# The place of each row's greatest entry, found through 22 segment maxima and one gathered segment

## The chip, the cores and the metric

One core of one Trainium2 chip runs the whole program in one launch. The metric is the device time of a run in microseconds (us), the median over repeated runs. Engines are written as in the profile: PE multiplies matrices (PEld loads its weights), DVE, ACT and POOL work on vectors, SP issues transfers, and POOL also issues the indirect transfers (gathers by a list of rows).

## The reference

The input is a table `x` of 2708 rows by 512 and a matrix `adj` of 2708 by 2708, all float32. Four layers follow one another, each with a layer norm and relu before it and `x` added after it. Only layers 0 and 1 matter for this change:

```python
h = jnp.maximum(_layernorm(x, axis=-1), 0.0)
# layer 0
mask = adj > 0
head = mask / jnp.maximum(jnp.sqrt(jnp.sum(mask * mask, -1, keepdims=True)), 1e-12)
inc = adj + head
x = x + (inc @ h) / jnp.sum(inc, -1, keepdims=True)
# layer 1, with h computed anew from x
a = jnp.maximum(adj, jnp.eye(n))
atts = queries @ keys.T / key_dim ** 0.5        # for each of 8 heads
atts = softmax(atts - 1e16 * (1.0 - a))
x = x + sum_over_heads(atts @ values @ Wo)
# layer 2: two graph convolutions with adj, relu, relu, then tanh of a product
# layer 3: the mask adj != 0 times a projection, over the column sums of the mask
```

Most entries of `adj` are zero, the others lie between 0.05 and 5.42, and the first rows and columns hold most of them. Layer 1's mask is multiplied by 1e16, so that in a row whose greatest and second greatest entries of `max(adj, I)` differ enough, the softmax is 1 at the place of the greatest entry and 0 elsewhere. The layer is then a lookup: each row takes the projected row that its greatest entry points to.

## The kernel before, in words

The rows are worked in 22 row tiles, 21 of 128 rows and a tail tile of 20. `tile_adj_preln_kernel` computes layer 0 in its first part, up to about 515 us; the layers after it have code of their own.

Layer 0 multiplies a dense first part of the adjacency by blocks, and gathers the rest. The rest of a row tile's columns is sparse, so the kernel finds which of them are non-zero at all (`count`, `rank_blocks`, `search`), fetches just these rows of the transposed adjacency by indirect transfers issued on POOL (`gather_adj`, L635, tiles `ac`), fetches the rows of the normalised table that belong to them (`gather_rows`, L654, tiles `h`), and lets PE add their products (L866, operands `inc` for dense blocks, `incl` for gathered ones). `incidence` makes these operands on DVE: L698 takes the mask part, L706 adds the entry.

`stats_to` runs ahead of PE. For each row tile it loads the tile's rows of `adj` whole (`load_slab`, a `slab` tile `ar` of 128 x 2708), forms the row's statistics with ACT (`row_norm`, `row_sum`: number of positive entries, sum, degree) and then calls `attended`, which finds the greatest and second greatest entry and the place of the greatest:

```python
nc.vector.tensor_max(ar[:n, cols], ar[:n, cols], ident[:n, :n])
nc.vector.max(tops[:n, m, :], ar[:n])
nc.vector.max_index(at_top[:n, m, :], tops[:n, m, :], ar[:n])
```

The first instruction puts the identity into the tile's diagonal block (L622), the second returns a row's eight greatest values (L623, MAX8), and the third the places of those eight (L624, which the profile shows as a load of the eight values, MATCH_VALUE_LOAD, and a search, FIND_INDEX8). Row tiles 0 to 5 (`LATE`) leave this out at first; their rows are loaded again in iterations 15 to 20 of the loop over row tiles, and `attended` is called one iteration after each load (L892-895).

`flags` (L278-288) later compares the two greatest values of each row and asks for a general attention path where they are too close; the rows of this input take the lookup. L914 copies the places into `idx`, by which layer 1's lookup gathers (L1172).

The main loop (L857-913) runs over the 22 row tiles: PE's sum, the scaling by the degree and the addition of `x` (L879), the layer norm of the result (`norm`, with the small operations L194 to L204), its transposition and projection one and two iterations later (`after`), then `stats_to` and `gathers_to` for tiles ahead. Each engine works its instructions in order, and POOL's gathers of all kinds share one queue. Tiles of the scratch pool have a set number of buffers; an instruction that writes one waits until the last reader of what was in it is done.

Of the kernel before, what the change touches and what calls it, by code (L numbers as in the profile page):

```python
# [9 lines left out]
FP = mybir.dt.float32  # L10
# [3 lines left out]
U32 = mybir.dt.uint32  # L14
U8 = mybir.dt.uint8
I32 = mybir.dt.int32
AF = mybir.ActivationFunctionType
ALU = mybir.AluOpType
AX = mybir.AxisListType
# [3 lines left out]
P = 128  # L23
LN_EPS = 1e-5
NORM_EPS = 1e-12
MASK_SCALE = 1e16
# [18 lines left out]
def kernel(  # L45
# [27 lines left out]
    nc = tc.nc  # L73

    N, D = x.shape
    H, _, DK = wk_d.shape
    NT = (N + P - 1) // P
    NFULL = N // P
# [4 lines left out]
    UNIT = 4  # L83
# [20 lines left out]
    ident = const.tile([P, P], FP, name="ident")  # L104
# [43 lines left out]
    idx = const.tile([P, NT], U32, name="idx")  # L148
# [16 lines left out]
    nc.gpsimd.memset(ones_b, 1.0)  # L165


    adj_units = bass.AP(adj_t.tensor, 0, [[UNIT, N * N // UNIT], [1, UNIT]])

    def span(t):  # L170
# [73 lines left out]
    with tc.tile_pool(name="l0_slab", bufs=2) as slabs, tc.tile_pool(  # L244
        name="l0_h", bufs=1
    ) as hp, tc.tile_pool(name="l0_w", bufs=2) as wp, tc.tile_pool(
        name="l0_acc", bufs=2, space=PSUM
    ) as ps_acc, tc.tile_pool(name="l0_small", bufs=1, space=PSUM) as ps_small, tc.tile_pool(
        name="l0_list", bufs=3, space=PSUM
    ) as ps_list, tc.tile_pool(name="l0_tr", bufs=1, space=PSUM) as ps_tr, tc.tile_pool(  # L250
        name="l0_y", bufs=1, space=PSUM
# [8 lines left out]

        idx_a = hp.tile([P, NT, NCH], U32, name="idx_a")

        tops = hp.tile([P, NT, 8], FP, name="tops")
        at_top = hp.tile([P, NT, 8], U32, name="at_top")
        cnts, sums_sgn, ends, caps = (
            hp.tile([P, NT], FP, name=name) for name in ("cnts", "sums_sgn", "ends", "caps")
        )
# [5 lines left out]
        if TAIL:  # L273
            nc.gpsimd.memset(tops[:, NFULL, :], 0.0)
            nc.gpsimd.memset(tops[:, NFULL, 0:1], 2.0)
            nc.gpsimd.memset(at_top[:, NFULL, :], 0)

        def flags():  # L278

            score = wp.tile([P, NT, 2], FP, name="score", bufs=1)  # L280
            nc.vector.tensor_scalar(
                score, tops[:, :, 0:2], 1.0, MASK_SCALE, op0=ALU.subtract, op1=ALU.mult
            )
            nc.vector.tensor_tensor(bad[:, :NT], score[:, :, 1], score[:, :, 0], ALU.is_ge)
            nc.vector.tensor_tensor(
                bad[:, BAD_NEG : BAD_NEG + NT], sums_sgn, cnts, ALU.not_equal
            )
            nc.vector.tensor_tensor(bad[:, BAD_MANY : BAD_MANY + NT], ends, caps, ALU.is_gt)
# [17 lines left out]
        nc.gpsimd.iota(place_i, pattern=[[P, NCH]], base=1, channel_multiplier=1)  # L306
        places = hp.tile([P, NCH], FP, name="places")
        nc.vector.tensor_copy(places, place_i)

        pending, pending_c = [], []  # L310

# [253 lines left out]
        def count_signs(m, last):  # L565

            sgn = slabs.tile([P, N], BF, name="sgn", bufs=GROUP)
            behind(sgn[:1, :1], last)
            nc.scalar.activation(sgn, slab[m], AF.Sign, accum_out=sums_sgn[:, m : m + 1])
            nc.scalar.activation(sgn, sgn, AF.Relu, accum_out=cnts[:, m : m + 1])  # L570
# [46 lines left out]
        def attended(m):  # L617

            n = rows(m)
            cols = slice(m * P, m * P + n)  # L620
            ar = slab.pop(m)
            nc.vector.tensor_max(ar[:n, cols], ar[:n, cols], ident[:n, :n])  # L622
            nc.vector.max(tops[:n, m, :], ar[:n])  # L623
            nc.vector.max_index(at_top[:n, m, :], tops[:n, m, :], ar[:n])  # L624

        gathers, gather_slot = {}, [0]

# [117 lines left out]
        normed, near, far = [0], [LEAD], [LEAD]  # L745
# [16 lines left out]
        def stats_to(m):  # L762


            while normed[0] <= order_n.index(m):
                t = order_n[normed[0]]
                do_next()
                load_slab(t)
                if normed[0] + 1 < NT:
                    load_slab(order_n[normed[0] + 1])  # L770
                row_norm(t)
                row_sum(t)
                if t == 0 or t % GROUP == GROUP - 1 or t >= NT - 2:
                    last_block = count(masks)
                    if t not in ZERO:
                        if dense_of(t):
                            rank_blocks(list(masks), last_block)
                        else:
                            flush_counts()
                            todo.append(partial(rank_rows, list(masks)))  # L780
                        todo.extend(partial(search, k) for k in masks)
                        do_next(0)
                    masks.clear()
                if t in LATE:
                    slab.pop(t)
                else:
                    attended(t)
                normed[0] += 1
# [65 lines left out]
        for m in range(NT):  # L854
            n = rows(m)
            if m + 1 < NT:
                load_x(m + 1)  # L857
            if m + 2 < NT and m + 2 >= LEAD and dense_of(m + 2):
                blocks[m + 2] = load_block(m + 2, tiles_d[: min(dense_of(m + 2), PIECE0)])
            flush()  # L860
            if LEAD <= m + 1 < NT:
                incs[m + 1] = incidence(m + 1)
            acc = ps_acc.tile([P, D], FP, name="acc")
            pairs = incs.pop(m)
            for i, (a, g) in enumerate(pairs):
                product = nc.tensor.matmul(  # L866
                    acc[:n], a, g, start=(i == 0), stop=(i == len(pairs) - 1)
                )
                first_of_sum = first_of_sum if i else product.ins
            if m + 1 < LEAD:  # L870
                stats_to(m + 1)
                incs[m + 1] = incidence(m + 1)
            if m > 1:
                with tc.issue_after(first_of_sum):
                    after(m - 2, None)
            if m:
                after(m - 1, hns.pop(m - 1))
            xt = xs.pop(m)
            nc.vector.scalar_tensor_tensor(  # L879
                xt[:n], acc[:n], row.pop(m)[1][:n], xt[:n], op0=ALU.mult, op1=ALU.add  # L880
            )
            hns[m] = wp.tile([P, D], FP, name="hn")
            norm(wp, xt, n, hns[m])
            store(m, xt)
            if normed[0] == NT:
                do_next(2 if NT - 8 < m < NT - 5 else 1)
            stats_to(min(2 * m + 6, m + 8, NT - 1))
            gathers_to(m + 2)

            step = m - (NT - 8)  # L890
            if 0 <= step < len(LATE):
                load_slab(LATE[step])  # L892
            if 0 < step <= len(LATE):
                count_signs(LATE[step - 1], xt[:1, :1])
                attended(LATE[step - 1])
            if m + 8 == NT + 1:
                todo.append(partial(rank_rows, list(range(1, LEAD))))
                todo.extend(partial(search, k) for k in range(1, LEAD))
            if m == NT // 2:
                load_scores(xt[:1, :1])  # L900
            if m == NT // 2 + 2:
                score_bound(xt[:1, :1])
            if m == NT - LEAD - 1:
                for t in range(1, LEAD):
                    gather_adj(t)
            if m == NT // 2 + 3:
                wr = load_w(wset, w1_d, "wr", lambda w: behind(w[:1, 0, :1], xt[:1, :1]))
            if m == NT // 2 + 5:
                w1 = split_w(
                    wset, wr, "wa", lambda w: behind(w[:1, :1], xt[:1, :1])  # L910
                )
                wr = load_w(wset, w3_d, "wr")
        flush()
        nc.vector.tensor_copy(idx, at_top[:, :, 0])  # L914
        degrees()
        after(NT - 2, None)
        after(NT - 1, hns.pop(NT - 1))
# [13 lines left out]
    ap = short.enter_context(tc.tile_pool(name="ap", bufs=2))  # L931
    wp = short.enter_context(tc.tile_pool(name="wp", bufs=2))
# [535 lines left out]
    for i in range(NT + 3):  # L1468
# [5 lines left out]
        if i < NT:  # L1474
            m = order_2[i]
            sums[m] = aggregated(m, second_parts, second_product, g2d, bias3)
            if m == 0:
                w = split_w(wsetb, wr, "wb")
# [48 lines left out]
    with tc.If(general > 0):  # L1527

        with tc.tile_pool(name="l0_g", bufs=2) as gp, tc.tile_pool(
            name="l0_gh", bufs=1  # L1530
        ) as hp, tc.tile_pool(name="l0_gps", bufs=2, space=PSUM) as ps:
            hs = []
            for t in range(NT):
                n = rows(t)
# [5 lines left out]
            for m in range(NT):  # L1540
                n = rows(m)
                cols = slice(m * P, m * P + n)
                ar = gp.tile([P, N], FP, name="ar")
# [40 lines left out]
        with tc.tile_pool(name="l1_qkv", bufs=1) as qkvp:  # L1584
# [6 lines left out]
            with tc.tile_pool(name="l1_pw", bufs=1) as pwp, tc.tile_pool(  # L1591
                name="l1_ph", bufs=2
            ) as php, tc.tile_pool(name="l1_px", bufs=3) as pxp, tc.tile_pool(
                name="l1_pps", bufs=2, space=PSUM
# [4 lines left out]
                for w, src in ((wk, wk_d), (wq, wq_d), (wv, wv_d)):  # L1599
                    for h in range(H):  # L1600
                        nc.sync.dma_start(
                            out=w[:, :, h * DK : (h + 1) * DK],
                            in_=src[h].rearrange("(c p) k -> p c k", p=P),
                        )
                for b in range(NB):
# [4 lines left out]
                    for t in tiles:  # L1610
                        n = rows(t)
# [21 lines left out]
                    for t in tiles:  # L1633
                        n = rows(t)
# [3 lines left out]
            with tc.tile_pool(name="l1_bias", bufs=2) as bp, tc.tile_pool(  # L1638
                name="l1_p", bufs=2
            ) as pp, tc.tile_pool(name="l1_pT", bufs=3) as ptp, tc.tile_pool(  # L1640
                name="l1_x", bufs=1
            ) as xp, tc.tile_pool(name="l1_st", bufs=4) as stp, tc.tile_pool(
                name="l1_s", bufs=2, space=PSUM
            ) as ps_s, tc.tile_pool(name="l1_t", bufs=2, space=PSUM) as ps_t, tc.tile_pool(
                name="l1_o", bufs=1, space=PSUM
            ) as ps_o, tc.tile_pool(name="l1_y", bufs=1, space=PSUM) as ps_y:
                SW = 2 * BLK
                for m in range(NT):
                    n = rows(m)
# [10 lines left out]
                    for h in range(H):  # L1660
                        oc, r0 = divmod(h * DK, P)
                        p = pp.tile([P, N], FP, name="p")
                        for s0 in range(0, N, SW):
                            sw = min(SW, N - s0)
                            s = ps_s.tile([P, SW], FP, name="s")
# [64 lines left out]
        with ExitStack() as gen:  # L1730

            atp = gen.enter_context(tc.tile_pool(name="at", bufs=2))
            wp = gen.enter_context(tc.tile_pool(name="wp", bufs=3))
            hp = gen.enter_context(tc.tile_pool(name="hp", bufs=2))
# [10 lines left out]
            w = load_w(wts, w_d, "w")  # L1745
# [79 lines left out]
            for t in range(NT):  # L1825
                n = rows(t)
# [10 lines left out]
            for block in range(NB):  # L1837
# [3 lines left out]
                for t in node_tiles(c0, nb):  # L1841
                    n = rows(t)
# [34 lines left out]
            for t in range(NT):  # L1877
                n = rows(t)
# [74 lines left out]
```

## Time and profile before

| | |
|---|---|
| median of 15 runs | 1427.94 us (1421.16 to 1440.8) |
| profiled execution | 1424.47 us, its span 1422.6 us |
| mean granted PE clock | 0.936 |
| PE busy | 1214.7 us (85%) |
| DVE busy | 924.7 us (65%), 1859 instructions |
| ACT busy | 693.4 us (49%) |
| POOL busy | 668.1 us (47%), 703 instructions |
| indirect transfers of layer 0 | 130 of `ac` (L635) and 111 of `h` (L654) |

The times beside the median are whole executions; the profile's times count from the start of its span. A line of the profile names the source line, the engine, the operation, what it writes and reads and the shape; in groups, "| busy, mean ns of one | idle time before, and what ended it" follow. "<- remote" means that the profile found no instruction that ended the wait. Busy shares are taken over the whole span, whereas layer 0 is the part up to about 515 us.

### The profile page before, as it was taken

How to read it: one execution, taken by the hardware profiler on the slowest of the kernel's cores; microseconds unless marked ns; L12 is line 12 of the kernel's file. 1: busy time of each engine (PE TensorE's matmuls, PEld its weight loads, DVE VectorE, ACT ScalarE, POOL GpSimd, SP SyncE). 2: the span in 40 equal slices, each digit the busy share in tenths (PEclk: the TensorE clock that was granted, in tenths of full speed). 3: DMA queues.
4: the chain of work that ended last, by engine and by line, in shares of the span. 5: the costliest groups of instructions: out<-in, count | busy, mean ns of one | idle time of the engine just before them, and what ended most of it. 6: DMA issues, size and time to landing. Idle time of an engine off the chain costs nothing. (4 is left out here: it accounts for less than half of the span.)

```text
span 1422.6 us, 15148 instructions
## 1 busy us (share of the span) xinstructions
PE 1214.7 (85%) x4223; PEld 720.8 (51%) x4223; DVE 924.7 (65%) x1859; ACT 693.4 (49%) x1098; POOL 668.1 (47%) x703
## 2 busy tenths in 40 slices
PE   4887976869686938999989999899999999959887
PEld 2332432324332416765655665466666766637665
DVE  4676984859698958953444445456677686736576
ACT  5875453647535546642333223244555554635453
POOL 2245475556557351106554543245444444066663
PEclk9988998889898978999999999999999999979899
DMA  9987887879868659727887888766666666487885
GB/s 343 349 292 229 320 273 240 265 236 310 274 202 308 243 188 330 246 90 260 267 288 239 275 261 258 261 198 199 220 187 203 217 192 204 134 315 250 261 245 169
DMA packets 179341, 349.92 MB, mean 246 GB/s; under 512 B 22794, under 2 KB 85524, under 8 KB 175516
## 3 DMA queue, kind: packets, MB, share of 16 engines
q1 hardware_dynamic: 131648, 201.72, 42.3%
q0 software_dynamic: 46032, 145.05, 32.2%
q10 hardware_dynamic: 1568, 2.10, 0.4%
q8 instruction: 35, 0.57, 0.2%
q14 instruction: 58, 0.48, 0.1%
HBM read 285.97 MB, written 62.82 MB: 245 GB/s over the span
## 5 line engine op out<-in xcount | busy, mean ns | idle before, releaser
L1110 PE MATMUL aggs<-gg,ac 128*128 128x512 f32 (+1 forms) x520 | 232.0, 596 | 3.3 <-DMA gg<-g1d,idx_g 2.6
L1047 POOL DMA_INDIRECT gg<-g2d,idx_g x130 | 138.8, 1068 | 196.1 <-PE aggs L1110 145.1
L1047 POOL DMA_INDIRECT gg<-g1d,idx_g x130 | 130.2, 1001 | 154.4 <-PE aggs L1110 81.1
L635 POOL DMA_INDIRECT ac<-in_adj_t_dram,idx_a x130 | 135.0, 1038 | 93.7 <-issue 36.3
L866 PE MATMUL acc<-h,inc 128*128 128x512 f32 (+1 forms) x276 | 140.3, 652 | 38.4 <-DVE inc L706 20.1
L1110 PEld LDWEIGHTS aggs<-gg,ac 128*128 128x128 f32 (+1 forms) x520 | 97.8, 189 | 113.6 <-issue 101.9
L654 POOL DMA_INDIRECT h<-h0d,idx_g x111 | 114.2, 1029 | 87.2 <-issue 32.8
L866 PE MATMUL acc<-h,incl 128*128 128x512 f32 (+1 forms) x222 | 108.0, 626 | 2.3 <-issue 2.3
L866 PEld LDWEIGHTS acc<-h,inc 128*128 128x128 f32 (+1 forms) x276 | 53.8, 207 | 99.6 <-issue 69.1
L176 PE MATMUL yacc<-wvo,hT 128*128 128x512 f32 (+1 forms) x176 | 85.5, 625 | 8.2 <-ACT hT L211 8.2
L1047 POOL DMA_INDIRECT gg<-hidr,idx_g x62 | 67.7, 1092 | 38.8 <-issue 18.3
L1075 DVE SCALAR_TENSOR_TENSOR ac<-ac,diag_c,bias 128x512 f32<-128x512 f32 x30 | 22.7, 755 | 91.8 <-DMA ac<-g1d 59.5
L1106 PE MATMUL agg<-ghi,a_hi 128*128 128x512 f32 x180 | 75.4, 419 | 0.0
L1106 PE MATMUL agg<-glo,a_lo 128*128 128x512 f32 x180 | 71.8, 399 | 3.5 <-ACT glo L225 3.5
L1106 PE MATMUL aggs<-gs,a_s 128*128 128x512 f32 x180 | 71.7, 399 | 1.3 <-DVE gs L222 1.3
L866 PEld LDWEIGHTS acc<-h,incl 128*128 128x128 f32 (+1 forms) x222 | 42.4, 198 | 52.1 <-issue 50.2
L990 DVE SCALAR_TENSOR_TENSOR v_lo<-pt,v_hi 128x512 fp32r<-128x512 f32 (+1 forms) x88 | 56.9, 656 | 16.0 <-ACT v_hi L989 12.6
L623 DVE MAX8 tops<-ar 128x8 f32<-128x2708 f32 (+1 forms) x22 | 65.3, 2970 | 0.0
L624 DVE FIND_INDEX8 at_top<-tops,ar 128x8 uint32<-128x2708 f32 (+1 forms) x22 | 65.3, 2968 | 0.0
L989 ACT ACTIVATE v_hi<-pt 128x512 fp32r<-128x512 f32 (+1 forms) x88 | 48.2, 575 | 29.5 <-PE pt L983 23.7
L176 PEld LDWEIGHTS yacc<-wvo,hT 128*128 128x128 f32 (+1 forms) x176 | 34.2, 198 | 52.4 <-issue 42.4
L1139 DVE SCALAR_TENSOR_TENSOR u<-aggs,u 128x512 f32<-128x512 f32 x42 | 28.8, 686 | 48.5 <-PE aggs L1110 43.6
(355 smaller groups left out, 2788.6 us busy)
## 6 DMA issues: line engine op xcount, KB each, us to landing
ar<-in_adj_dram SPq DMA_DIRECT2D x27, 1354.0 KB
raw<-in_adj_t_dram SPq DMA_DIRECT2D x92, 192.0 KB
slot<-x SPq DMA_DIRECT2D x41, 256.0 KB
at<-in_adj_t_dram SPq DMA_DIRECT2D x26, 256.0 KB
h<-in_x_dram SPq DMA_DIRECT2D x21, 256.0 KB
h0d<-h POOLq DMA_DIRECT2D x21, 256.0 KB
xt<-in_x_dram SPq DMA_DIRECT2D x21, 256.0 KB
x<-xt SPq DMA_DIRECT2D x21, 256.0 KB
```

Of the source, the lines that this page charges most:

```text
L176: nc.tensor.matmul(acc[:n], hT[:, c, :n], w[:, c, :], start=(c == 0), stop=(c == NCD - 1))
L623: nc.vector.max(tops[:n, m, :], ar[:n])
L624: nc.vector.max_index(at_top[:n, m, :], tops[:n, m, :], ar[:n])
L635: nc.gpsimd.indirect_dma_start(out=ac[:, c, :n], out_offset=None, in_=adj_units, element_offset=dense_of(m) * P * N + m * P, in_offset=bas ...
L654: nc.gpsimd.indirect_dma_start(out=g, out_offset=None, in_=h0d[:, :], in_offset=bass.IndirectOffsetOnAxis(ap=index_g(m)[:, c : c + 1], axi ...
L866: product = nc.tensor.matmul(acc[:n], a, g, start=(i == 0), stop=(i == len(pairs) - 1))
L989: nc.scalar.activation(hi[d], pt[d], AF.Relu, scale=UP)
L990: nc.vector.scalar_tensor_tensor(lo[d], pt[d], 0.0, hi[d].bitcast(FP), op0=ALU.max, op1=ALU.subtract)
L1047: nc.gpsimd.indirect_dma_start(out=gs[c], out_offset=None, in_=gd[:, :], in_offset=bass.IndirectOffsetOnAxis(ap=index_g(m)[:, c : c + 1], ...
L1106: turn(nc.tensor.matmul(acc[:n], a[:k, i, :n], b[:k], start=st, stop=sp))
L1110: nc.tensor.matmul(mixed[:n], a, g, start=(c == 0 and not dense_of(m)), stop=(c == len(chunks) - 1),)
L1139: done = nc.vector.scalar_tensor_tensor(u[:n], mixed[:n], EPS12, u[:n], op0=ALU.mult, op1=ALU.add)
```

## The change

For a full row tile, `attended` no longer runs MAX8 and FIND_INDEX8 over 2708 columns. It takes the maximum of each of 21 segments of 128 columns with one reduction and of the last 20 columns with another, then runs MAX8 and FIND_INDEX8 over these 22 values. From the number of the greatest segment it works out where that segment begins, in units of four columns (`begin`, at most the last place from which 128 columns remain), and the unit of each row in memory (`place`). The tail tile keeps the two whole passes, through small tiles.

A new function `look` is called before each `attended`. Where three windows wait, or windows wait and no segment does, it takes the oldest window: it puts the identity into the window if this is the tile's own diagonal block, runs MAX8 and FIND_INDEX8 over its 128 columns, and combines value and place into `tops` and `at_top`. Then, where a segment waits, it issues one indirect transfer on POOL, which fetches for each of the tile's 128 rows its own window of 128 columns from `adj` (64 KB). So a window is looked into three row tiles after it was fetched. What still waits at the end of the loop is looked into before L914. The main loop calls `look` once more in iterations without an `attended`, once all row tiles have their statistics.

Lines as in the diff's new side, cut to the core ("..." marks what is left out):

```diff
+    row_units = bass.AP(adj.tensor, 0, [[UNIT, N * N // UNIT], [1, UNIT]])
...
-        tops = hp.tile([P, NT, 8], FP, name="tops")
-        at_top = hp.tile([P, NT, 8], U32, name="at_top")
+        tops = hp.tile([P, NT, 2], FP, name="tops")
+        at_top = hp.tile([P, NT], U32, name="at_top")
...
+        row_i = hp.tile([P, 1], I32, name="row_i")
+        nc.gpsimd.iota(row_i, pattern=[[0, 1]], base=0, channel_multiplier=N // UNIT)
+        row_unit = hp.tile([P, 1], FP, name="row_unit")
+        nc.vector.tensor_copy(row_unit, row_i)
...
             nc.vector.tensor_max(ar[:n, cols], ar[:n, cols], ident[:n, :n])
-            nc.vector.max(tops[:n, m, :], ar[:n])
-            nc.vector.max_index(at_top[:n, m, :], tops[:n, m, :], ar[:n])
+            if n < P:
...
+                return
+            segs = wp.tile([P, NT], FP, name="segs", bufs=1)
+            near_w = NFULL * P
+            nc.vector.tensor_reduce(
+                segs[:, :NFULL],
+                ar[:, :near_w].rearrange("p (s w) -> p s w", w=P),
+                AX.X,
+                ALU.max,
+            )
+            nc.vector.tensor_reduce(segs[:, NFULL:], ar[:, near_w:], AX.X, ALU.max)
+            peaks = wp.tile([P, 8], FP, name="peaks", bufs=5)
+            nc.vector.max(peaks, segs)
+            best = wp.tile([P, 8], U32, name="best", bufs=1)
+            nc.vector.max_index(best, peaks, segs)
+            begin = wp.tile([P, 1], FP, name="begin", bufs=5)
+            nc.vector.tensor_scalar(
+                begin, best[:, 0:1], float(P // UNIT), float((N - P) // UNIT), op0=ALU.mult, op1=ALU.min
+            )
+            place = wp.tile([P, 1], U32, name="place", bufs=2)
+            nc.vector.tensor_scalar(place, begin, row_unit[:, 0:1], None, op0=ALU.add)
+            segments.append((m, begin, place, peaks))
+
+        segments, windows = [], []
+
+        def look():
+
+            if windows and (len(windows) == 3 or not segments):
+                m, begin, win, peaks = windows.pop(0)
+                own = wp.tile([P, 1], FP, name="own_seg")
+                nc.vector.tensor_scalar(
+                    own, begin, float(m * P // UNIT), None, op0=ALU.is_equal
+                )
+                nc.vector.scalar_tensor_tensor(
+                    win, ident, own[:, 0:1], win, op0=ALU.mult, op1=ALU.max
+                )
+                high = wp.tile([P, 8], FP, name="high", bufs=1)
+                nc.vector.max(high, win)
+                where = wp.tile([P, 8], U32, name="where", bufs=1)
+                nc.vector.max_index(where, high, win)
+                nc.vector.tensor_max(tops[:, m, :], peaks[:, 0:2], high[:, 0:2])
+                nc.vector.scalar_tensor_tensor(
+                    at_top[:, m : m + 1], begin, float(UNIT), where[:, 0:1],
+                    op0=ALU.mult, op1=ALU.add,
+                )
+            if segments:
+                m, begin, place, peaks = segments.pop(0)
+                win = wp.tile([P, P], FP, name="win", bufs=3)
+                nc.gpsimd.indirect_dma_start(
+                    out=win,
+                    out_offset=None,
+                    in_=row_units,
+                    element_offset=m * P * N,
+                    in_offset=bass.IndirectOffsetOnAxis(ap=place[:, 0:1], axis=0),
+                )
+                windows.append((m, begin, win, peaks))
...
                     masks.clear()
+                look()
                 if t in LATE:
...
                 count_signs(LATE[step - 1], xt[:1, :1])
+                look()
                 attended(LATE[step - 1])
+            elif normed[0] == NT:
+                look()
...
         flush()
-        nc.vector.tensor_copy(idx, at_top[:, :, 0])
+        while segments or windows:
+            look()
+        nc.vector.tensor_copy(idx, at_top)
```

More of the change, by code (lines that the diff above doesn't have):

```diff
@@ L275 @@
             nc.gpsimd.memset(tops[:, NFULL, 0:1], 2.0)
-            nc.gpsimd.memset(at_top[:, NFULL, :], 0)
+            nc.gpsimd.memset(at_top[:, NFULL:], 0)
         def flags():
@@ L281, in flags @@
             nc.vector.tensor_scalar(
-                score, tops[:, :, 0:2], 1.0, MASK_SCALE, op0=ALU.subtract, op1=ALU.mult
+                score, tops, 1.0, MASK_SCALE, op0=ALU.subtract, op1=ALU.mult
             )
@@ L622, in attended @@
             nc.vector.tensor_max(ar[:n, cols], ar[:n, cols], ident[:n, :n])
-            nc.vector.max(tops[:n, m, :], ar[:n])
-            nc.vector.max_index(at_top[:n, m, :], tops[:n, m, :], ar[:n])
+            if n < P:
+                high = wp.tile([P, 8], FP, name="high", bufs=1)
+                nc.vector.max(high[:n], ar[:n])
+                where = wp.tile([P, 8], U32, name="where", bufs=1)
+                nc.vector.max_index(where[:n], high[:n], ar[:n])
+                nc.vector.tensor_copy(tops[:n, m, :], high[:n, 0:2])
+                nc.vector.tensor_copy(at_top[:n, m : m + 1], where[:n, 0:1])
+                return
@@ new lines, in look @@
+        def look():
[8 more added lines that the diff above has]
+                )
+                high = wp.tile([P, 8], FP, name="high", bufs=1)
+                nc.vector.max(high, win)
+                where = wp.tile([P, 8], U32, name="where", bufs=1)
+                nc.vector.max_index(where, high, win)
+                nc.vector.tensor_max(tops[:, m, :], peaks[:, 0:2], high[:, 0:2])
+                nc.vector.scalar_tensor_tensor(
+                    at_top[:, m : m + 1],
+                    begin,
+                    float(UNIT),
+                    where[:, 0:1],
+                    op0=ALU.mult,
+                    op1=ALU.add,
+                )
[10 more added lines that the diff above has]
+                windows.append((m, begin, win, peaks))
```

## The prediction

> **What bounds the kernel now.** I read the table by stage first, because the change touches only layer 0, the first 515 us. Columns: stretch and length, then busy time of PE, PEld, DVE, ACT and POOL with instruction counts, granted PE clock, DMA share, GB/s.
>
> ```profile
> 86.00:391.00 305.00, 239.89 (x708) 106.21 (x707) 223.11 (x430) 166.20 (x229) 178.91 (x184) 0.89 0.81 269
> 391.00:427.00 36.00, 29.36 (x76) 13.85 (x75) 32.70 (x57) 13.61 (x22) 19.91 (x14) 0.91 0.65 203
> 427.00:462.00 35.00, 21.58 (x54) 10.06 (x53) 31.44 (x49) 19.00 (x31) 28.03 (x20) 0.80 0.87 307
> 462.00:498.00 36.00, 35.30 (x93) 15.44 (x92) 33.71 (x56) 19.96 (x24) 14.43 (x15) 1.00 0.67 244
> ```
>
> The reader is to see that from 391 to 498 DVE is busy 90 to 94% and can be the bound, while before that it has 27% of free time and after 522 no operation of the change runs. Next, what the engines waited for in layer 0 (us in total, times, longest):
>
> ```profile
> DVE rk L399 <- ACT counts L343: 40.1, 4, 15.4
> PE list L403 <- DVE rk L399: 36.7, 5, 12.7
> ACT counts L341 <- remote: 36.5, 3, 17.5
> ...
> PE acc L866 <- DVE inc L706: 20.1, 2, 13.4
> ```
>
> The free time of DVE before 391 (82 us) is for more than half four stalls (about 209-216, 239-254, 303-315 and 361-372; 45 us) in which PE, DVE and ACT hardly move. The timeline shows what runs in them:
>
> ```profile
> 247.94 0.95 POOL L654 DMA_INDIRECT h<-h0d,idx_g  x1 [0.30 <-issue]
> 249.19 0.95 POOL L654 DMA_INDIRECT h<-h0d,idx_g  x1 [0.30 <-issue]
> 253.70 0.58 ACT L341 CAST counts<-list 128x512 bf16<-128x512 f32 x1 [17.49 <-remote]
> ...
> 254.44 0.76 DVE L399 TENSOR_SCALAR_CACHE_REDUCE rk<-counts 128x581 f16<-128x581 bf16 x1 [15.38 <-ACT counts L343]
> ```
>
> POOL issues gathers back to back (201-213, 228-250, 295-312, 355-370), and each stall ends shortly after that run has landed. Why, the trace doesn't say ("remote" names no one), so the coupling is a reading. Elsewhere POOL is 20 to 30 us ahead of PE's use of the rows.
>
> Only in the other wait, PE for L706, is DVE itself late. The 13.42 us one:
>
> ```profile
> 445.09 2.95 DVE L623 MAX8 tops<-ar 128x8 f32<-128x2708 f32 x1
> ...
> 448.68 2.96 DVE L624 FIND_INDEX8 at_top<-tops,ar 128x8 uint32<-128x2708 f32 x1
> ...
> 455.17 0.54 DVE L706 TENSOR_TENSOR inc<-inc,at 128x384 f32<-128x384 f32 x1
> ...
> 455.77 2.08 PE L866 MATMUL acc<-h,inc 128*128 128x512 f32 x2 [13.42 <-DVE inc L706]
> ```
>
> The two passes that the change touches stand in DVE's order in front of the operand that PE wants.
>
> **The change on DVE.** Prices come from these groups (busy us, mean ns):
>
> ```profile
> L623 DVE MAX8 tops<-ar 128x8 f32<-128x2708 f32 (+1 forms) x22 | 65.3, 2970 | 0.0
> L624 DVE FIND_INDEX8 at_top<-tops,ar 128x8 uint32<-128x2708 f32 (+1 forms) x22 | 65.3, 2968 | 0.0
> ...
> L1514 DVE TENSOR_REDUCE some<-bad 128x1 f32<-128x67 f32 x1 | 0.2, 214 | 0.0
> ```
>
> Removed from each full tile: 2.97 (MAX8) + 0.08 (value load, L624's 79 ns) + 2.97 (FIND_INDEX8) = 6.02 us. Added: a reduction of 2688 elements, which no row shows. Index searches of 1941 and 2709 f16 elements took 2.170 and 2.972 us, so 1.044 ns an element and 0.14 fixed; with that slope the reduction costs 2.95, and the one reduction in the trace (67 elements, 0.214, against 0.21 by the slope) fits. Its ends: 1.0 us if it ran at the 0.34 ns an element of L423's one-source pass (1940 in 0.66), 5.8 if at the 2.14 of a scan (2708 in 5.78); the reduction row puts it at 2.95. Then: reduction of 20, 0.16; MAX8 and FIND_INDEX8 of 22, 0.17 each by the slope, and a value load, 0.08; `begin` 0.16 (L585); `place` 0.20 (L201). Sum 3.89. Three row tiles later, in `look`: `own` 0.16; 128x128 product 0.28 (L595's 276 ns); MAX8 and FIND_INDEX8 of 128, 0.28 each; value load 0.08; `tops` 0.14 (L546); `at_top` 0.21 (L612). Sum 1.43. So 5.32 for 6.02: 0.70 us less a tile, end to end. These are durations, not pitches: an independent successor starts 0.06 to 0.09 us before its predecessor ends (L706 at 201.72 after a MAX8 that ends at 201.81), a dependent one 0.03 after (a MAX8 ending at 427.85, its value load at 427.88). With eleven instructions more, the saving lies between 0.4 and 1.5. I take 0.9, 19 us over 21 tiles; the tail tile keeps both passes.
>
> The Trainium skill ("VectorE: DVE Perf Modes", The DRAIN you can't avoid, and Rules for kernel authors) says that the next operation doesn't start until the pipe has emptied, advises fewer operations, and has a reduction at single speed as the slowest one, to be restructured away. The starts above disagree on the first point where operations are independent; by the page alone the saving would be at most the 0.70, 15 us in all, which argues against the change.
>
> Most of the 19 us is off the path. DVE ends last before PE at six attends by their starts: 198.8 (PE then waits 3.04), 351.9, 380.8, 424.9, 445.1 and 502.9. Six times 0.9 is 5 us. What is late next at 445: the splits L217 and L222 and the scan, unchanged; so no more than the saving comes back.
>
> **The change on POOL.** It adds 21 indirect gathers, one a full tile, in the form of L635's: 0.94 us and 0.30 to the next, 1.25 each, 26 us on POOL (668 us busy, 47%). Outside the four runs this is covered by the 20 to 30 us lead; without it, all 26 would show. Within them, one or two gathers lengthen each run: 4 x 1.25 x (1 to 2) = 5 to 10 us; I take 7. If the coupling is false it is 0, the lower end. A gather also waits for its `place`, and behind it in POOL's order stand the row gathers of L635 and L654. POOL runs behind DVE there: `idx_a` of row tiles 8 to 17 was written 12 to 30 us before the first gather by it (tile 8: 175.1 and 201.5), so I add nothing for this wait. The transfers, 21 x 64 KB = 1.4 MB of 350, are small.
>
> One gather took 6.40 us instead of 0.94 while DVE ran the f16 scan of 411.89 (5.78); beside MAX8 and FIND_INDEX8 gathers kept 0.94. I expect the reduction to behave like those two. The Trainium skill ("SBUF — State Buffer", Who interferes with whom) has a reduction on this chip never lock GpSimd out, which would keep 0.94; no run shows it yet.
>
> **The look** queues on DVE a wait for a gather issued three tiles, 40 to 60 us, earlier; gathers land about 2.6 us after the last issue (POOL's list store waits 2.62 at 492.4). Nothing expected; behind a wait would stand the next `inc` and `incl`, and PE behind those.
>
> **The tail.** The last three looks can't lag. POOL works in order, and the last three gathers come behind the nineteen of tiles 1 and 2, whose list store ends at 516.04. 516.04 + 3 x 1.25 + 2.6 landing + 1.43 look + 0.16 copy of `idx` = 524.0, against 522.44, where the gather by `idx` (L1172) starts today, held by the y store and not by `idx` (ready at 509.2). That is +1.6. If the third `place`, which has two buffers, holds row tile 21's normalisation on DVE behind it, I get about +6. 0 to 6, taken +3.
>
> **Sum.** -5 +7 +3 = +5. Against the profiled execution (span 1422.6, 1424.47 in all) that is 1429.5; the median of the 15 runs, 1427.94, lies 3.5 above it, so the forecast for the median is 1433. About 0.3%, 4.3 us, is what a measurement of this kernel can tell from no change.
>
> **The rivals.** *DVE's saving lands.* With 1.4 us a tile on ten tiles (391-502 and the three before PE's waits), -14, no coupling and a tail of +2: 1416 (1406 to 1423). For it: DVE 90 to 94% busy from 391 to 498; the overlap of neighbours. Against: PE is 98% busy in 462-498, and 427-462 holds scans and splits. It decides if the gap between small operations is under 0.05 us and the stalls don't grow.
>
> *The order waits.* `place` has two buffers, so DVE can write a tile's `place` only when POOL has read that of two tiles before, whose gather was issued about one attend earlier. Attends start 13 to 33 us apart, POOL lags 12 to 30: where a long lag meets a short step, DVE waits up to 30 - 13 = 17 us with `inc` behind it and PE behind that. One such wait, 12 taken, on top of the sum: +17, 1445 (1437 to 1460). For it: the lag is in the trace. Against: step and lag are both near 20 on average, and a wait inside the four stalls costs nothing. It decides from a lag longer than the step.
>
> *It does nothing measurable*: the saving and the gathers are both hidden, 1428 (1424 to 1432).
>
> **How the numbers follow.** Forecast case (1427 to 1440) 0.47, saving lands 0.34, order waits 0.15, nothing 0.04. The forecast case has about 0.13 within 4.3 us and 0.34 above. Faster: 0.32 of the second. Same: 0.13 + 0.04 + 0.02 = 0.19. Slower: 0.34 + 0.15 = 0.49. The range 1413 to 1447 leaves out the ends of the second and third case, some 0.2; the forecast's own is 1427 to 1440.
>
> **What the profile after would show.** L623's and L624's groups give way to a reduction of about 2.95 us and small operations summing to 2.4 us a tile; DVE busy falls by 10 to 31 us; POOL rises by 20 us of busy time in 21 more gathers; the stalls near 215, 254, 315 and 372 last longer; L1172 starts 2 to 6 us later against row tile 21's end. Wrong would be: stalls of unchanged length, the reduction far from 2.95, DVE waiting for `win` or for POOL at `place`, or PE's 13.42 us wait shrinking by more than 3 us.

## The result and the profile after

The changed kernel took 1455.69 us (median of 9 runs, 1447.25 to 1461.97) against 1428.71 (47 runs): 1.0186 times the kernel before, 95% interval 1.0159 to 1.0213, so about 27 us slower. The profiled execution took 1444.04 us, 12 less than the median; its span is 1442.2, 19.6 longer than before. The direction was forecast, the size (+5) was not, and the time lies above the forecast's range, which ended at 1447.

In the traces all of it is lost in layer 0. Row tile 21's sum (L879, now L950) starts at 517.3 us instead of 498.6, the first gather of layer 1 at 543.3 instead of 522.4, and the rest takes as long as before. The page's first section and the groups that took the place of the two whole passes:

```profile
PE 1221.8 (85%) x4223; PEld 727.2 (50%) x4223; DVE 897.2 (62%) x2093; ACT 693.6 (48%) x1098; POOL 686.1 (48%) x725
```

```profile
L639 DVE TENSOR_REDUCE segs<-ar 128x21 f32<-128x2688 f32 x21 | 61.8, 2943 | 6.0 <-issue 6.0
...
L668 DVE SCALAR_TENSOR_TENSOR win<-ident,own_seg,win 128x128 f32<-128x128 f32 x21 | 7.3, 347 | 42.6 <-DMA win<-in_adj_dram,place 33.2 <-issue 8.7 <-DVE win L668 0.6
L672 DVE MAX8 high<-win 128x8 f32<-128x128 f32 x21 | 5.9, 282 | 2.5 <-DVE win L668 1.3 <-DVE rstd L200 1.1
L674 DVE FIND_INDEX8 where<-high,win 128x8 uint32<-128x128 f32 x21 | 5.9, 282 | 0.0
```

DVE is busy 27.5 us less, as the change means it to be. But the first instruction of the look, L668, has 42.6 us of idle time in front of it. No whole pass had any in the kernel before. The list of waits in layer 0 names what ended them:

```profile
DVE win L668 <- DMA win<-in_adj_dram,place: 33.2, 5, 8.9
...
DVE win L668 <- issue: 8.7, 2, 8.1
```

Seven waits, 41.9 us; the trace of the tile `win` puts all seven down to the gathered window. Five of them (30.4 us) come before row tile 21's sum; the last two (8.9 and 2.6 us) come after it, where the last windows are looked into. The timeline shows one of them on DVE, and POOL beside it:

```profile
503.40 0.15 DVE L676 SCALAR_TENSOR_TENSOR at_top<-begin,where 128x1 uint32<-128x1 f32 x1
511.33 0.35 DVE L668 SCALAR_TENSOR_TENSOR win<-ident,own_seg,win 128x128 f32<-128x128 f32 x1 [7.78 <-DMA win<-in_adj_dram,place]
511.60 2.95 DVE L639 TENSOR_REDUCE segs<-ar 128x21 f32<-128x2688 f32 x1
514.47 0.74 DVE L950 SCALAR_TENSOR_TENSOR xt<-acc,deg,xt 128x512 f32<-128x512 f32 x1
```

```profile
506.33 0.97 POOL L705 DMA_INDIRECT ac<-in_adj_t_dram,idx_a  x1 [2.62 <-DMA lst<-ac]
507.61 0.95 POOL L705 DMA_INDIRECT ac<-in_adj_t_dram,idx_a  x1 [0.30 <-issue]
508.86 0.94 POOL L687 DMA_INDIRECT win<-in_adj_dram,place  x1 [0.30 <-issue]
```

DVE comes to the look of row tile 0 at 503.6, before POOL has issued its gather at all. Behind the wait stand the next reduction and row tile 20's sum, L950. Not every wait delays PE by its length: during this one PE is busy all the time, while behind the one that ends at 147.04 PE waits 4.07 us for an operand that DVE makes behind L668 (`inc`, L768). This is not the order of the source, where the look of row tile 0 comes after the reductions of tiles 1 and 2. When the program is built, each engine's instructions are put in an order of the builder's own (I call this the planner), and the look was moved up to right behind its gather: the seven looks that wait start 1.5 to 6.5 us after the gather's issue is over, the other fourteen 3 to 61 us after.

### The profile page after: what moved, and what is told of

The parts are those of the page before. It is cut to its first block, busy times and chain, and to the rows that moved or that the text cites. A ratio compares the mean times of both kernels' runs of the same rounds, so it can differ in the third digit from the quotient of the medians.

```text
span 1442.2 us, 15407 instructions
## 1 busy us (share of the span) xinstructions
PE 1221.8 (85%) x4223; PEld 727.2 (50%) x4223; DVE 897.2 (62%) x2093; ACT 693.6 (48%) x1098; POOL 686.1 (48%) x725
## 5 line engine op out<-in xcount | busy, mean ns | idle before, releaser
L937 PE MATMUL acc<-h,inc 128*128 128x512 f32 (+1 forms) x276 | 140.0, 650 | 19.6 <-issue 14.5
L937 PE MATMUL acc<-h,incl 128*128 128x512 f32 (+1 forms) x222 | 103.2, 614 | 0.0
L1151 DVE SCALAR_TENSOR_TENSOR ac<-ac,diag_c,bias 128x512 f32<-128x512 f32 x30 | 22.6, 753 | 87.2 <-DMA ac<-g1d 51.2
L639 DVE TENSOR_REDUCE segs<-ar 128x21 f32<-128x2688 f32 x21 | 61.8, 2943 | 6.0 <-issue 6.0
L1086 PE MATMUL main<-wb,v_hi 128*128 128x512 f32 (+1 forms) x176 | 57.2, 447 | 3.7 <-ACT v_hi L1065 3.7
L1069 DVE SCALAR_TENSOR_TENSOR v_s<-v_lo,v_hi 128x512 fp32r<-128x512 f32 (+1 forms) x88 | 57.9, 664 | 0.8
```

What stands on the lines that cost most here:

```text
L639: nc.vector.tensor_reduce(segs[:, :NFULL], ar[:, :near_w].rearrange("p (s w) -> p s w", w=P), AX.X, ALU.max,)
L937: product = nc.tensor.matmul(acc[:n], a, g, start=(i == 0), stop=(i == len(pairs) - 1))
L1069: nc.vector.scalar_tensor_tensor(s[d], lo[d].bitcast(FP), SHIFT, hi[d].bitcast(FP), op0=ALU.mult, op1=ALU.add)
L1086: nc.tensor.matmul(acc[:n], a[:, c, :n], b[:, c, :], start=first and c == 0, stop=last and c == NCD - 1,)
```

## The experiments

Each kernel was run beside the kernel before, on the same chip; the runs went to five chips. On four of them the kernel before took 1431 to 1437 us, on one 1354. So ratios are given, and compared within a chip first.

**Look held behind the newest reduction** (that chip of 1354 us), the first of four kernels run there.

```diff
-            nc.vector.tensor_reduce(segs[:, :NFULL], ...)
+            latest[0] = nc.vector.tensor_reduce(segs[:, :NFULL], ...).ins
...
                 m, begin, win, peaks = windows.pop(0)
-                own = ...      # and the look's other operations
+                with tc.issue_after(latest[0]):
+                    own = ...
```

> The changed kernel, with each look's seven DVE operations held behind the segment reduction of the newest row tile, so that DVE meets them three tiles after the gather, as the source orders them, and not where the planner puts them. Theory W (DVE stands in order, 42 us in 7 waits, for windows that have not landed, because the look comes 2 to 7 us after the gather's issue): these waits go and 15 to 25 us come back, 1430 to 1440. Theory P (the 21 gathers lengthen POOL's runs, as predicted): nothing comes back, 1452 to 1460. Theory T (only the last three looks at the end cost): they still stand at the end, 1445 to 1455.

1.0074 (1.005 to 1.0098). DVE now comes to 15 of the 21 looks 20 us or more after the gather. Three waits for windows are left, in the drains (24.9 us), and a new one shows in the waits:

```profile
DVE win L669 <- DMA win<-in_adj_dram,place: 24.9, 3, 11.8
...
DVE place L655 <- DMA win<-in_adj_dram,place: 18.5, 4, 9.4
```

The second line is the rival of the prediction: `place` has two buffers, and DVE waits for POOL to have read the older. In the changed kernel itself `place` waited only 2.6 us. The ratio points to W, but the changed kernel was not run on this chip, so how much came back here isn't shown.

**Segments only: no gather, no look.**

```diff
-                own = ...  # seven operations on the window
+                nc.vector.tensor_copy(tops[:, m, :], peaks[:, 0:2])
+                nc.vector.tensor_copy(at_top[:, m : m + 1], place)
...
-                win = ...; nc.gpsimd.indirect_dma_start(out=win, ...)
```

> The changed kernel without gather and without look: the place written is that of the segment's start, the greatest values are those of the segment maxima; the 22 segment maxima, MAX8 and FIND_INDEX8 over 22 stay, and two small copies a tile. It leaves out the place inside the segment. W, P and T all expect the loss to go and DVE's saving (about 45 us of busy time against the kernel before) to show in part: 1410 to 1425. If instead the new order of all other instructions is what costs (theory R), it stays at 1440 or more.

> The kernel without gather and without look once more, beside the next three on one chip; like the first time it leaves out the place inside the segment. If DVE's saving is worth the same where the chip shows the long stalls of the first traces, 0.990 to 0.995 of before; if the stalls hide it, 0.997 to 1.003.

0.9925 (0.9898 to 0.9952) on the fast chip and 0.9897 (0.9855 to 0.9939) on another. So DVE's saving is worth 10 to 15 us, and the new segment operations, in the order built for this kernel, cost nothing. That speaks against theory R but doesn't rule it out, because each kernel gets an order of its own.

**The kernel before with 21 unread gathers.**

```diff
             nc.vector.max_index(at_top[:n, m, :], tops[:n, m, :], ar[:n])
+            if n == P:
+                segments.append(m)
...
+                nc.gpsimd.indirect_dma_start(out=win, ..., ap=row_unit[:, 0:1])
```

> The kernel before, whole passes kept, plus 21 unread gathers of 128 windows of 128 columns on POOL where the changed kernel issues them, with a constant list of places, so that nobody waits for them. P: each run of POOL gathers grows by one or two, 1436 to 1445. W and T: nothing, 1425 to 1433.

> The kernel before with 21 unread gathers once more. P said that each POOL run in a stall grows: 1.004 to 1.008 on a chip that shows the stalls, and 1.000 as before on one that doesn't. W: 0.998 to 1.002 on either.

0.9999 (0.9981 to 1.0016) and 0.9986 (0.9951 to 1.0022), the second on a chip whose trace shows standstills like those of the first profile. But the gathers don't run where the expectation puts them. With a constant list nothing ties them to `attended`, and the planner moved all 21 ahead of the loop. The gathers of the second of these runs, and those of the changed kernel:

```profile
L641 POOL DMA_INDIRECT win<-in_adj_dram,row_unit x21: 944/965/1477, 22.8 to 73.0; - x21
```

```profile
L687 POOL DMA_INDIRECT win<-in_adj_dram,place x21: 941/946/1385, 113.1 to 532.6; - x21
```

After 86 us POOL does what it did before (busy 253.1 us for 251.5 between 86 and 520). So the two runs show that 21 gathers cost nothing at the start of the kernel; they say nothing on the same gathers inside the loop, and don't test P.

**Last three row tiles with whole passes.**

```diff
-            if n < P:
+            if n < P or m in ZERO:
```

> The changed kernel, but row tiles 0, 1 and 2, the last ones to be looked into, take the two whole passes again; 18 tiles keep segments and windows. T (the last three windows are gathered behind POOL's last 19 gathers and each holds DVE): the ten us that the trace shows lost between row tiles 19 and 21 come back, 1443 to 1448. W: as T, since three of the seven waits (19 us) go with them, and the four earlier waits stay. P: 3 of 21 gathers less, 1452 to 1456.

1.0228 (1.0204 to 1.0251), slower than every theory said. Its waits go the same way:

```profile
DVE win L668 <- DMA win<-in_adj_dram,place: 57.7, 10, 9.9
```

The planner made another order, and DVE waits ten times for the 18 windows left. T, that the end alone costs, falls; the waits and the loss are both larger here than in the changed kernel (on other chips).

**The changed kernel on a second chip**, as the base of the three that follow.

> The changed kernel itself, on the chip of the following experiments. W (DVE's waits for windows cost, wherever it runs): 1.015 to 1.023 of the kernel before, with 7 to 10 waits of DVE for windows, 35 to 60 us in all. If part of the 1.0186 belonged to the stalls that the first chip's traces show and this chip's don't (theory S, a chip's own trouble), the ratio is under 1.010.

1.0182 (1.015 to 1.0214), with 49.1 us in eight waits for windows: the loss is the same on another chip. S falls. This trace has no complete standstill of PE, DVE and ACT over 3 us between 86 and 522 us, the first chip's has 19.5 us of them, so the loss doesn't hang on these.

**A stand-in for the window**: gathers as they are, but the look works on a fixed tile.

```diff
+                win = stand_in
                 nc.vector.scalar_tensor_tensor(
                     win, ident, own[:, 0:1], win, op0=ALU.mult, op1=ALU.max
                 )
```

> The changed kernel with its 21 gathers issued as they are, but each look's operations work on a fixed 128x128 tile in place of the gathered window, so that DVE never waits for a gather; the place inside the segment is left out by that. W: everything lost is the wait, so 0.992 to 1.002 of before. Theory L (the look's 14 small operations themselves, or where they stand, delay DVE's products): 1.008 or more.

> The stand-in kernel once more, as the base of the next two (it leaves out the place inside the segment, as they do): 1.001 to 1.006 of before on any chip.

1.0035 (1.0011 to 1.0058) beside the 1.0182, and 1.0013 (0.9985 to 1.004) on another chip. Every operation and every gather is still there, and the wait is gone, as the group shows:

```profile
L671 DVE SCALAR_TENSOR_TENSOR stand_in<-ident,own_seg,stand_in 128x128 f32<-128x128 f32 x21 | 7.2, 342 | 0.1
```

0.1 us idle in place of 42.6, and on the same chip 0.0147 x 1431 = 21 us back. W had put the first at 1.002 at most, which its interval includes; L's 1.008 or more lies outside it. This experiment speaks most clearly for the larger part. It changes one more thing: with nothing to tie a look to its gather, the planner puts six of the 21 looks ahead of theirs, so a part of the 21 us can belong to the other order.

**Held, and a window kept until its buffer is wanted; then five buffers for `place` too.**

```diff
-            if windows and (len(windows) == 3 or not segments):
+            if windows and (last or len(windows) == 3 and segments):
```

```diff
-            place = wp.tile([P, 1], U32, name="place", bufs=2)
+            place = wp.tile([P, 1], U32, name="place", bufs=5)
```

> As the first experiment (looks held behind the newest reduction, 1.0074), and in the loop a window is looked into only when its buffer is wanted for the next segment, so that windows 18, 19 and 20 no longer are drained one after another in iterations 13 and 14. W: the two waits of 4.9 and 8.2 us at 333 and 342 go, 1.000 to 1.004. Against W: 1.007 or more.

> The same with five buffers for place instead of two. In the first experiment DVE waited 18.5 us in 4 waits at place for POOL to have read the one of two tiles before. If these waits are on the path, 0.992 to 0.999 of before, as near to the 0.9925 without look and gather as the look's operations allow; if they are hidden, the same as the last one, 1.000 to 1.004.

1.0081 (1.0051 to 1.0111) and 1.013 (1.0094 to 1.0165). The first misses its mark: W had been given 1.000 to 1.004, and 1.007 or more was to count against it. In its trace the looks stand 9 us or more behind their gathers all through the loop, and DVE waits for no gathered window there. Two waits for windows are left, at the very end (DVE's timeline):

```profile
531.52 0.35 DVE L669 SCALAR_TENSOR_TENSOR win<-ident,own_seg,win 128x128 f32<-128x128 f32 x1 [13.26 <-issue]
...
535.05 0.35 DVE L669 SCALAR_TENSOR_TENSOR win<-ident,own_seg,win 128x128 f32<-128x128 f32 x1 [1.89 <-DMA win<-in_adj_dram,place]
```

They are those of row tiles 1 and 2, whose gathers POOL issues at 528.9 and 532.5, behind its last gathers by L706. The first gather of layer 1 starts 29 us after row tile 21's sum there. So against the 1.0182 on the same chip 1% comes back when the waits of the loop go, in a kernel that still computes everything; the waits of the loop are not the whole loss. `place` waits only 0.3 us in that trace, so five buffers had nothing to take away; that the second kernel is the slower one shows how far another order alone can move the time, if their overlapping intervals show anything.

**Where the rest sits**: held, with row tiles 0 to 2, then all six late tiles, by whole passes.

```diff
-            if n < P:
+            if n < P or m in ZERO:    # the other kernel: m in LATE
...
-                nc.vector.max(high[:n], ar[:n])
+                latest[0] = nc.vector.max(high[:n], ar[:n]).ins
```

> The held looks with windows kept until their buffer is wanted (1.0081 on the second chip), and row tiles 0, 1 and 2 with the two whole passes. In the trace of that kernel the first gather by idx starts 29 us after row tile 21's sum, against 24 in the kernel before: that tail, 5 us, should go, and 1.002 to 1.006 remain. If the tail is not the rest of the loss, 1.007 or more.

> Held looks, windows only for row tiles 6 to 20, the six late tiles with whole passes. No window or place is gathered behind POOL's last gathers, no wait at the end: if the rest of the loss sits in the late tiles, 0.995 to 1.001 of before; if it sits in the look's operations between row tiles 9 and 20, 1.002 to 1.008.

1.0043 (1.0012 to 1.0074) and 1.0026 (0.9995 to 1.0056). (The second also looks into a kept window at each late tile but the first.) The second is the best kernel here with windows that still computes the whole reference; it can't be told from the kernel before and doesn't beat it. The end was part of the rest: from row tile 21's sum to layer 1's first gather the two take 18 and 21 us, where the held kernel took 29 on another chip.

**The look without gathers, and the stand-in held.**

```diff
-                win = ...; nc.gpsimd.indirect_dma_start(out=win, ...)
-                windows.append((m, begin, win, peaks))
+                windows.append((m, begin, None, peaks))
```

> The stand-in kernel without its 21 gathers; the look's operations stay. If the gathers beside the rest cost, once DVE's order is the new one (theory P again): 0.990 to 0.996. If the look's 30 us of DVE operations are what is paid (theory L): as the stand-in, 1.000 to 1.005.

> The look's operations without gathers once more (the place inside the segment is left out, as in the next two), as the base: 0.983 to 0.992 of before.

> The stand-in kernel with looks held behind the newest reduction, windows kept until their buffer is wanted. No wait for a window is left, only the order differs from the stand-in and only the wait for the gather from the held kernel (1.0081 on the second chip). Theory L: as the stand-in, 1.001 to 1.006. If the held place itself costs (the looks stand between the reduction and PE's operands): 1.006 to 1.010.

Without gathers 0.987 (0.9812 to 0.9929) and 0.9918 (0.9875 to 0.9962): the same as without the look as well, so the look's operations cost nothing that shows, and L falls. On the first of these two chips the stand-in with its gathers took 1.0013: there the 21 gathers, issued in the loop, cost 0.0143 x 1432 = 20 us. The 0.987 is even below the 0.990 to 0.996 that P was given here: the gathers cost in this order. Held, the stand-in took 1.0079 (1.0045 to 1.0113). It has no window to wait for, in the loop or at the end, and is 0.7% above the stand-in that isn't held on the same chip, so holding a look has a price of its own; order alone moves the time by that much. It doesn't fit well with the 1.0026 and 1.0043 of held kernels that do read their windows, on another chip; what the price is for stays open.

**What of a gather costs**: a constant list instead of `place`; a plain load instead of the gather.

```diff
-                    in_offset=bass.IndirectOffsetOnAxis(ap=place[:, 0:1], axis=0),
+                    in_offset=bass.IndirectOffsetOnAxis(ap=row_unit_i[:, 0:1], axis=0),
```

```diff
-                nc.gpsimd.indirect_dma_start(out=win, ..., ap=place[:, 0:1], ...)
+                nc.sync.dma_start(out=win, in_=adj[m * P : m * P + P, :P])
```

> The stand-in kernel with its 21 gathers by a constant list instead of place, so that POOL never waits for DVE's place and DVE's place never for POOL. If the dependence is what costs: 0.984 to 0.993, as without gathers. If POOL's 26 us in this order cost: 0.998 to 1.005, as the stand-in.

> The stand-in kernel with each gather replaced by a plain load of 64 KB on SP's queue, no list and no POOL. If POOL's gathers cost: 0.984 to 0.993. If the traffic costs: 0.998 or more.

0.9968 (0.9935 to 1.0) and 0.9964 (0.9933 to 0.9995), beside 0.9918 without any on the same chip. Both lie between the two expectations, and their intervals overlap those of either side. Nor do they test what they were meant to: the gathers with a constant list are all issued between 22.6 and 65.6 us, the plain loads between 99 and 225, where the gathers of the changed kernel run from 113 to 533. It stays open how the gathers' cost divides into the dependence on `place`, POOL's instructions, the traffic, and the order that the planner makes of each kernel.

## Why the prediction was wrong in size

The step that failed is the look: "Nothing expected", because "a gather issued three tiles, 40 to 60 us, earlier" would have landed. That lag was read from the source. In the instruction order on the chip it wasn't there: DVE stood in seven looks for 41.9 us. The stand-in puts this term at 21 us on one chip; from the mean of both stand-ins (1.0024) to 1.0182 it is 0.0158 x 1430 = 23 (both with the change of order that a stand-in brings). The text had named what would stand behind such a wait, the operands and then PE; only its price was set at nothing.

Against the other terms:

- DVE's own prices were right. Durations a tile were to sum to 3.89 and 1.43; they are 2.943 + 0.942 = 3.88 and 1.43, with the reduction, which no row of before showed, at 2.94 for 2.95.
- The saving in DVE's busy time was taken as 19 us within 10 to 31; it is 27.5, or 1.31 a tile. The durations of all DVE instructions together fell by 14.7 us (1043.7 to 1029.1), which is the 0.70 a tile of the sum; the rest is overlap, because small operations overlap their neighbours more than I took. The prediction read the Trainium skill ("VectorE: DVE Perf Modes", The DRAIN you can't avoid) as a bound of 15 us. The same section says that a next operation that isn't held starts earlier, and with that this trace agrees: DVE's instructions overlap by 131.8 us in all, for 119.1 before.
- Of the saving, -5 was to land. Without the look and its gathers 1.0% lands, about 15 us: the step "no more than the saving comes back" at six attends was too narrow. PE's 20.1 us of waiting for DVE's L706 before its sums has shrunk to 1.3 in the changed profile (L776), a sign that the text had put down against its forecast; of the group's 19.6 us of idle time 14.5 are "issue".
- POOL's 21 gathers were +7 by way of longer standstills. In the order with looks they are worth 19 us (0.0130 x 1430; 1.0024 less the 0.9894 of the two runs without gathers, means over chips). The traces don't show longer standstills as the way: in complete standstills of PE, DVE and ACT over 3 us, between 86 and 522 us, the traces have 33.9 us before, 19.5 in the changed kernel and none in it on the second chip, 9.4 and 19.8 in the stand-ins, 21.2 and 14.2 in the two without gathers. So the size was too small and the mechanism isn't borne out; how the gathers cost stays open, since in the kernels that were to isolate them they, or the loads in their place, ran earlier.
- The tail was +3. From row tile 21's sum to the first gather of layer 1 it is 26.0 us for 23.8 before, +2.2.

So -15, +19 and +23 stand for DVE, gathers and look where -5, +7 and 0 were written (the tail's 2 is in them). Each is the difference of two neighbouring kernels, taken partly across chips, so they add up to the 1.0182 (26 us) by construction; that is no check of their parts. Without the look's waits the measured terms come to about +3, near the forecast's +5, but only because a saving and a cost were both sized too small by about 10 us. That nearness is luck, and so in part is the direction. The rival "the order waits" was the nearest: DVE, in order, waits for POOL, and its interval, 1437 to 1460, holds the time. It named the wrong buffer: `place` waited 2.6 us, `win` 41.9. (Its bound of 17 us took attends to start 13 to 33 us apart; in the trace of before they start 7.7 to 36.4 apart.) A late window was in the text as a sign against the forecast, and should have been a case with a price.

On a gather beside a reduction the row and the Trainium skill ("SBUF — State Buffer", Who interferes with whom) agree: 28 gathers of layer 0 lie wholly beside a reduction L639 (one of them a window gather) and took 0.943 to 0.973 us. The longest window gather, 1.385 us, ran beside a scan, L411.

## What to carry to other kernels

A lag written in the source is a lag only if the built order keeps it. Before a transfer's cost is set at nothing because its reader comes later, look up where the reader stands in the instruction order of its engine, or hold it there, and price the wait as the time of the transfer plus its queue. An engine relieved of 27 us of work is no gain where a new input makes it stand for 42. And an experiment that frees an operation of what it depended on may move it: before reading the result, look up in the trace where the operation ran.

## What the runs showed of the chips

The same kernel differs between chips by more than the change does: the kernel before took 1354 us on one chip and 1431 to 1437 on four. The kernel with unread gathers was profiled on the first and on one of the four, at granted clocks of 0.95 and 0.933. Its sum of row tile 21 starts at 441.1 on the one and 498.4 on the other, so most of the difference lies in layer 0. The waits there hold, on the slower chip only, lines such as

```profile
ACT counts L347 <- remote: 27.8, 2, 17.2
```

On the faster one the list of waits of layer 0 holds no line that ends in "remote", and neither do those of the other three kernels that ran there. Such waits are thus a matter of the chip. Complete standstills, on which the prediction built a term, go less by the chip: the changed kernel on the second chip has 88 us of "remote" waits between 86 and 520 and no standstill over 3 us. What ends these waits stays open. In the second stand-in trace PE's sums end at 246.8 and POOL then issues gathers alone until 257.3:

```profile
256.33 0.95 POOL L708 DMA_INDIRECT ac<-in_adj_t_dram,idx_a  x1 [0.31 <-issue]
259.85 0.58 ACT L347 CAST counts<-list 128x512 bf16<-128x512 f32 x1 [15.47 <-remote]
259.99 0.69 DVE L771 SCALAR_TENSOR_TENSOR inc<-at,rb 128x512 f32<-128x512 f32 x1 [12.83 <-remote]
```

ACT and DVE go on 2.6 us after the last gather's issue, while PE's last results before the standstill were there by 246.8.
